# Summing scan blocks over their states in four column groups of TensorE

## The chip, the cores and the metric

The kernel runs on one core of a Trainium2 chip. The metric is device time in microseconds (us), the median of several runs. A core has TensorE (PE; PEld is its weight load), VectorE (DVE), ScalarE (ACT), GpSimd (POOL) and SyncE (SP), which issues most DMAs. Each engine works through its own instructions in order and waits on semaphores for the others.

## The reference, cut to what matters

The program is two layers: a hybrid of a state space model, convolutions and attention, and then an attention layer with a mixture of experts. The change concerns only the selective scan in the first layer, done for four channel groups `nb` of each of four images `b`:

```python
def selective_scan(u, dt, Bm, Cm, A, Dp):
    dA = jnp.exp(dt[..., None] * A)                  # N x 128 channels x 16 states
    dBu = (dt * u)[..., None] * Bm[:, :, None, :]
    def step(h, inp):
        dA_t, dBu_t, C_t = inp
        h = dA_t * h + dBu_t
        return (h, jnp.einsum('bds,bs->bd', h, C_t)) # sum over the 16 states
    ...
    return ys.transpose(1, 0, 2) + u * Dp
```

N is 1024 tokens. For each channel and state a first-order recurrence runs over the tokens; its result is multiplied by C and summed over the 16 states.

## The kernel before, in words

One (nb, b) pair is called a group here, and `order` lists the 16 groups. A group has 128 channels by 16 states, 2048 recurrences; a block is 128 of them (8 channels by 16 states), one per partition, with 1024 tokens along the free dimension. So a group has NJ = 16 blocks and the scan NBLK = 256. Block t is block j = t % 16 of group n = t // 16.

The scan is a loop written out by hand (L808 to L837) in which turn t issues, in this order:

- DVE: the product of dBu with B (L813), then the recurrence into a buffer `hs` (`tensor_tensor_scan`, L816); POOL: `hs` times C, in place (L817)
- in turn j = 2, DVE and POOL close the previous group: `gated` (L479 reads the sum `pY`; L480)
- PE: `select(t + 2)` (L770), which spreads 8 rows of dt * u over 128 partitions into the PSUM tile dBu; there are two such tiles, so it must wait until the recurrence of block t has read the one that it takes
- PE: `add_up(t - 2)` (L778), the sum over states: two matmuls (one for each half of the 1024 tokens) of `hs` with a 128 x 128 matrix of zeros and ones cut out of `strip`. It puts the block's 8 channels into rows 8j to 8j + 7 of `pY`, adds nothing to the other rows, and accumulates over the 16 blocks; `pY` has one PSUM buffer
- SP: `fetch(t + 4)` (L758) brings 8 rows of dt, spread over 128 partitions, into `dA`; ACT: `decay(t + 3)` (L763) makes exp(dt * A) of it
- one of the steps of the next group's preparation, each at its own j: projections on PE (L400 in turns 11 to 14, L411 in turn 0, L457 in turns 8 and 9), activations on ACT, L422 (turn 3) and L429 (turn 5) on DVE, L426, L434, L439 and L444 on POOL
- in turns 6, 7 and 10: `project_out` of the previous group on PE (L487), `store` on DVE (L493), `gate` (L472)

A float32 matmul of 512 columns stands in the trace as two records of PE. The buffers `hs` come from the pool `scan`, of four buffers, so block t takes the buffer of block t - 4; `dA` has five. Before the scan a planner (`Plan`) orders the group norm and layer norm of the four images and the first group's preparation; the images lie in `xs`, of which images 0 and 1 use the four `hs` buffers and images 2 and 3 have tiles of their own in the pool `lnA`. After the scan a second plan runs everything else.

Of the kernel before, what the change touches and what calls it, by code (L numbers as in the profile page):

```python
# [10 lines left out]
F32 = mybir.dt.float32  # L11
# [4 lines left out]
PSUM = bass.MemoryType.PSUM  # L16

B, C, HH, WW = 4, 256, 32, 32
N = HH * WW
NP = N + 2  # L20
P = 128
CT = C // P
NT = N // P
NB, DM, DIN, DS, DTR, K = 4, 64, 128, 16, 4, 4
# [3 lines left out]
DB, XL = P // DS, K - 1  # L28
# [288 lines left out]
def body(tc, g, out):  # L317
    nc = tc.nc
    act, mm = nc.scalar.activation, nc.tensor.matmul
# [3 lines left out]
    def pool(name, bufs, **kw):  # L323
        return tc.tile_pool(name=name, bufs=bufs, **kw)

    with pool("const", 1) as cp, pool("dram", 1, space=bass.MemoryType.DRAM) as drp, contextlib.ExitStack() as late:
# [13 lines left out]
        strip = cst[:, c0 + TT + NTILE + 1 :]  # L340
# [24 lines left out]
        for b in range(B):  # L365
            t = xmp.tile([P, CT, XL + N + 1], F32, tag=f"xm{b}", name=f"xm{b}")
# [3 lines left out]
        NJ = DIN // DB  # L370
        order = [(nb, b) for b in range(B) for nb in range(NB)]
        NBLK = NJ * len(order)
        with pool("mconst", 1) as mc, pool("front", 1) as fp, pool("dts", 2, space=bass.MemoryType.DRAM) as dsp, pool(
# [119 lines left out]
                stt(xb, xb, V("skip")[rows_out], state[n]["po"][rows_out], ALU.mult, ALU.add)  # L493

            state = {}
            with pool("scan", 4) as sp, pool("yps", 1, space=PSUM) as yps, pool("dps", 2, space=PSUM) as dps, pool("lnA", 1) as wp:


                pre = Plan()
# [3 lines left out]
                pre.banks = [t[:, h] for t in first for h in HALVES] + [third[:, 0:512]]  # L503
                pg = third[:, 512 : 512 + 2 * B * CT].rearrange("p (b i k) -> p b i k", b=B, i=2)
                add, pre.spare, pre.slack, pre.split = pre.add, (2, 3), 700, True
                xs = [[sp.tile([P, N], F32, tag="hs", name="hs") for k in range(CT)] for b in range(2)]
                for b in range(2, B):
                    t = wp.tile([P, CT, N], F32, tag=f"xs{b}", name=f"xs{b}")
                    xs.append([t[:, k] for k in range(CT)])
                convr = sp.tile([P, N], F32, tag="dA", name="dA", bufs=5).rearrange("p (t k d) -> p t k d", t=CT, k=K)  # L510
# [241 lines left out]

                dAs, dBus, hss = {}, {}, {}

                def fetch(t):
                    if t < NBLK:
                        dAs[t] = sp.tile([P, N], F32, tag="dA", name="dA", bufs=5)
                        nc.sync.dma_start(out=dAs[t], in_=state[t // NJ]["ds"][t % NJ].unsqueeze(0).to_broadcast([DS, DB, N]))  # L758

                def decay(t):  # L760
                    if t < NBLK:
                        c = order[t // NJ][0] * NJ + t % NJ
                        act(dAs[t], dAs[t], AF.Exp, scale=aneg[:, c : c + 1])  # L763

                def select(t):
                    if t < NBLK:
                        j = t % NJ
                        dBus[t] = dps.tile([P, N], F32, tag="dBu", name="dBu")
                        for h in HALVES:
                            mm(dBus[t][:, h], pick[:, j % 4], state[t // NJ]["U"][:, j // 4, h], start=True, stop=True)  # L770

                def add_up(t):
                    if 0 <= t < NBLK:
                        r, j, hs = state[t // NJ], t % NJ, hss.pop(t)
                        if j == 0:
                            r["pY"] = yps.tile([P, N], F32, tag="y", name="pY")
                        for h in HALVES:
                            mm(r["pY"][:, h], strip[:, P - DB - j * DB : 2 * P - DB - j * DB], hs[:, h], start=j == 0, stop=j == NJ - 1)  # L778

                fronts = [front(n) for n in range(1, len(order))]  # L780
                fronts = [None] + fronts
# [8 lines left out]
                for t in range(4):  # L790
                    add("SP", 900, lambda t=t: fetch(t), ["ds"], [("dA", t)], lag=3000)
                add("ACT", 2400, lambda: decay(0), [("dA", 0), "aneg"], [("dA", 0)])
                add("PE", 1720, lambda: select(0), [("U", q, t) for q in range(3) for t in range(4)] + ["pick"], [("dBu", 0)])
                for t in range(1, 3):
                    add("ACT", 1150, lambda t=t: decay(t), [("dA", t), "aneg"], [("dA", t)])
                add("PE", 1720, lambda: select(1), [("U", q, t) for q in range(3) for t in range(4)] + ["pick"], [("dBu", 1)])
                with pre.beside(-1, -1, low=True):
                    for b in range(1, B):
# [8 lines left out]
                with tc.manual_schedule():  # L807
                    for t in range(NBLK + 9):  # L808
                        n, j = t // NJ, t % NJ
                        if t < NBLK:  # L810
                            r = state[n]
                            dBu = dBus.pop(t)
                            tt(dBu, dBu, r["B"], ALU.mult)  # L813

                            hs = hss[t] = sp.tile([P, N], F32, tag="hs", name="hs")
                            nc.vector.tensor_tensor_scan(hs, dAs.pop(t), dBu, 0.0, ALU.mult, ALU.add)  # L816
                            nc.gpsimd.tensor_tensor(hs, hs, r["C"], ALU.mult)  # L817
                        if j == 2 and n > 0:
                            gated(n - 1)
                        select(t + 2)  # L820
                        add_up(t - 2)
                        fetch(t + 4)
                        decay(t + 3)
                        for ahead in (1, 2):
                            if n + ahead < len(order):
                                for i, step in fronts[n + ahead]:
                                    if i == j - (ahead - 1) * NJ:
                                        step()
                        for i, step in behind:
                            if i == t:  # L830
                                step()
                        if n > 0 and j == 6:
                            project_out(n - 1)
                        if n > 0 and j == 7:
                            store(n - 1)
                        if n < len(order) and j == 10:
                            gate(n)  # L837
# [13 lines left out]
        with pool("sets", 1) as wp, pool("work", 1) as kp, pool("ps2", 1, space=PSUM) as ps:  # L851
# [830 lines left out]
            def experts(plan, *parts):  # L1682
# [20 lines left out]
                for j, (t, i, w) in enumerate(order):  # L1703
# [62 lines left out]
                    if adds:  # L1766
                        adds.pop()()
                    adds.append(add_up)
                adds.pop()()

# [41 lines left out]
            for i in range(B * NT + 2):  # L1812
                b, unit = i // NT, (i - 2) // HT
# [25 lines left out]
        with pool("fin", 3) as fp, pool("rows", 1) as yp, pool("pfin", 4, space=PSUM) as pf:  # L1839
# [5 lines left out]
            for u in range(2 * B):  # L1845
                b, half = u // 2, u % 2
# [20 lines left out]
```

## Time and profile before

| What | us |
|---|---|
| median of three runs (3322.93 to 3326.98) | 3326.42 |
| the profiled execution, its own time | 3332.46 |
| its span, first to last instruction | 3330.7 |
| the scan, first L816 to the end of the last | 104.4 to 1197.8 |
| busy in the span: PE, DVE, ACT, POOL | 2907, 2077, 1513, 1223 |
| busy in the scan: PE, DVE, ACT, POOL | 891, 957, 573, 775 |

The page gives for each group of instructions the line, the engine, the operation, what is written from what, the shapes and the count; behind the bar stand busy time in us and the mean of one in ns; behind the second bar the idle time of the engine just before them, with what ended it. "DVE hs L816 <- PE pY L778" reads: DVE stood before L816 until PE had finished an instruction of L778. PEclk is the granted clock of TensorE as a share of full speed; over the scan it is 0.93.

### The profile page before, as it was taken

How to read it: one execution, taken by the hardware profiler on the slowest of the kernel's cores; microseconds unless marked ns; L12 is line 12 of the kernel's file. 1: busy time of each engine (PE TensorE's matmuls, PEld its weight loads, DVE VectorE, ACT ScalarE, POOL GpSimd, SP SyncE). 2: the span in 40 equal slices, each digit the busy share in tenths (PEclk: the TensorE clock that was granted, in tenths of full speed). 3: DMA queues.
4: the chain of work that ended last, by engine and by line, in shares of the span. 5: the costliest groups of instructions: out<-in, count | busy, mean ns of one | idle time of the engine just before them, and what ended most of it. 6: DMA issues, size and time to landing. Idle time of an engine off the chain costs nothing. (4 is left out here: it accounts for less than half of the span.)

```text
span 3330.7 us, 38748 instructions
## 1 busy us (share of the span) xinstructions
PE 2907.4 (87%) x15274; PEld 1693.4 (51%) x15274; DVE 2077.2 (62%) x2347; ACT 1513.0 (45%) x2086; POOL 1223.0 (37%) x763
## 2 busy tenths in 40 slices
PE   7787788878888668998889989989899999899997
PEld 4333333333333224555555554655555656689996
DVE  5789888888888954746496478557364445511112
ACT  3646445554455423545673574565443333311111
POOL 0677767667767730000000010000002222556662
PEclk7899999998999988999999989999999999999998
DMA  3566555656557630000000000000000000465455
GB/s 125 133 159 160 152 145 149 167 145 156 143 150 170 153 113 0 1 1 1 26 1 1 26 1 1 1 14 1 1 13 7 13 7 14 117 193 131 117 124 157
DMA packets 92872, 265.50 MB, mean 80 GB/s; under 512 B 18182, under 2 KB 36086, under 8 KB 89360
## 3 DMA queue, kind: packets, MB, share of 16 engines
q1 hardware_dynamic: 64000, 198.46, 22.7%
q0 software_dynamic: 26512, 60.35, 7.1%
q10 hardware_dynamic: 2176, 4.19, 0.3%
q8 instruction: 121, 1.98, 0.2%
q14 instruction: 63, 0.52, 0.1%
HBM read 291.70 MB, written 42.80 MB: 100 GB/s over the span
## 5 line engine op out<-in xcount | busy, mean ns | idle before, releaser
L817 POOL TENSOR_TENSOR hs<-hs,bc 128x1024 f32<-128x1024 f32 x256 | 602.1, 2357 | 277.1 <-DVE hs L816 276.9
L816 DVE TENSOR_TENSOR_SCAN hs<-dA,dBu 128x1024 f32<-128x1024 f32 x256 | 585.4, 2287 | 73.8 <-PE pY L778 44.0
L778 PE MATMUL pY<-hs,const 128*128 128x512 f32 x1024 | 530.1, 643 | 15.6 <-DVE u L479 12.8
L763 ACT ACTIVATE dA<-dA,aneg 128x1024 f32<-128x1024 f32 x256 | 287.4, 1144 | 331.6 <-DMA dA<-ds 331.1
L1082 DVE TENSOR_REDUCE nm<-s 128x1 f32<-128x1024 f32 x256 | 301.6, 1219 | 203.4 <-PE s L1077 202.7
L1087 ACT ACTIVATE pr<-s,nm 128x1024 f32<-128x1024 f32 x256 | 284.9, 1116 | 196.9 <-DVE nm L1082 194.7
L1101 PE MATMUL k<-const,pr 128*128 128x128 f32 x2048 | 301.1, 291 | 72.8 <-ACT pr L1087 49.1
L1172 POOL TENSOR_TENSOR b<-b,misc 128x1024 f32<-128x1024 f32 x16 | 36.4, 2299 | 893.3 <-DVE misc L1168 835.0
L1101 PEld LDWEIGHTS k<-const,pr 128*128 128x128 f32 x2048 | 234.1, 147 | 191.8 <-issue 82.4
L770 PE MATMUL dBu<-U,pick 96*128 96x512 bf16 x512 | 162.7, 401 | 186.3 <-DVE hs L816 182.4
L813 DVE TENSOR_TENSOR dBu<-dBu,bc 128x1024 f32<-128x1024 f32 x256 | 311.8, 1218 | 4.0 <-PE dBu L770 3.9
L778 PEld LDWEIGHTS pY<-hs,const 128*128 128x128 f32 x1024 | 208.4, 205 | 204.4 <-issue 165.6
L1077 PE MATMUL s<-b,b 32*128 32x512 f32 x1024 | 286.9, 648 | 3.3 <-ACT pr L1087 3.3
L1107 ACT COPY pT<-k 128x512 f32<-128x512 f32 x320 | 175.8, 593 | 173.0 <-PE k L1101 171.8
L1742 PE MATMUL s<-pT,b 128*128 128x128 f32 x1920 | 230.0, 276 | 3.4 <-DMA b<-we,intse 2.9
L1742 PEld LDWEIGHTS s<-pT,b 128*128 128x128 f32 x1920 | 226.1, 192 | 8.6 <-ACT pT L1745 4.0
L770 PEld LDWEIGHTS <-pick 96*128 96x128 bf16 x512 | 41.8, 99 | 370.3 <-issue 303.6
L1107 DVE COPY pT<-k 128x512 f32<-128x512 f32 x192 | 131.6, 686 | 99.7 <-PE k L1101 85.4
L1746 DVE TENSOR_TENSOR pT<-pT,s 128x512 f32<-128x512 f32 x72 | 49.4, 687 | 228.2 <-ACT pT L1745 228.1
L1121 PE MATMUL k<-pT,b 128*32 128x128 f32 x4096 | 152.2, 290 | 17.9 <-DVE pT L1107 14.8
L1121 PEld LDWEIGHTS k<-pT,b 128*32 128x32 f32 x4096 | 113.1, 115 | 74.4 <-issue 31.1
L1077 PEld LDWEIGHTS s<-b,b 32*128 32x128 f32 x1024 | 102.4, 190 | 91.8 <-issue 76.5
(434 smaller groups left out, 4430.4 us busy)
## 6 DMA issues: line engine op xcount, KB each, us to landing
dA<-ds SPq DMA_DIRECT2D x256, 512.0 KB, 4.8
dq<-parts SPq DMA_DIRECT2D x15, 768.0 KB, 3.3
U<-dq SPq DMA_DIRECT2D x45, 256.0 KB, 4.1
ds<-dt SPq DMA_DIRECT2D x16, 512.0 KB, 3.0
b<-x SPq DMA_DIRECT2D x4, 1024.0 KB, 7.2
acc<-pr SPq DMA_DIRECT2D x8, 512.0 KB, 5.8
xm<-x SPq DMA_DIRECT2D x4, 1024.0 KB, 5.0
tokens<-pr SPq DMA_DIRECT2D x8, 512.0 KB, 2.9
```

The lines of the kernel that those rows point to most:

```text
L763: act(dAs[t], dAs[t], AF.Exp, scale=aneg[:, c : c + 1])
L778: mm(r["pY"][:, h], strip[:, P - DB - j * DB : 2 * P - DB - j * DB], hs[:, h], start=j == 0, stop=j == NJ - 1)
L813: tt(dBu, dBu, r["B"], ALU.mult)
L816: nc.vector.tensor_tensor_scan(hs, dAs.pop(t), dBu, 0.0, ALU.mult, ALU.add)
L817: nc.gpsimd.tensor_tensor(hs, hs, r["C"], ALU.mult)
L1077: mm(S[i][:, HALVES[h]], qT[rr, qt * P : (qt + 1) * P], kT[rr, HALVES[h]], start=True, stop=True)
L1082: "DVE", 1220, lambda i=i, u=u: nc.vector.tensor_reduce(nms[u], S[i], AX.X, ALU.max, negate=True),
L1087: "ACT", 1330, lambda i=i, u=u, hd=hd: act(prs[u % 4], S[i], AF.Exp, bias=nms[u], scale=1.0, accum_out=rss[b % 2][:, k, qt, hd : hd + 1]), ...
L1101: nc.tensor.transpose(bank.t[:, j * P : (j + 1) * P], prs[u][:, c0 : c0 + P], ident)
L1107: lambda dst=dst, bank=bank, on_act=on_act: (nc.scalar.copy if on_act else nc.vector.tensor_copy)(dst, bank.t),
L1121: mm(bank.t[i * HD : (i + 1) * HD, 0:P], v[:, 4 * jh + j, hd * HD : (hd + 1) * HD], pTs[m][jh][:, i, j * P : (j + 1) * P], start=j == 0, s ...
L1742: mm(p12[:, a, c], wbufs[w][:, o : o + P], xT[:, k], start=k == 0, stop=k == CT - 1)
```

## The change

It has three parts. The sum over states is done for four blocks at once: `add_up` does nothing until the fourth block of a set, and then issues eight matmuls (two halves, four blocks), each with 32 columns of `strip` instead of 128, written to the 32 rows of `pY` that belong to block i of the set. Matmuls to different 32-row strips of the output stand in different column groups of TensorE. For that, the blocks of a set must lie 32 channels apart, so blocks are worked off in the order 0, 4, 8, 12, 1, 5, 9, 13 and so on (`which`), and `fetch`, `decay` and `select` take their rows, scales and selections in that order. Since the results of a set must all be kept until then, the pool `scan` has six buffers instead of four; the two more hold image 2 during the norm, in place of its own tile.

`add_up(t - 2)` is still called in turn t, so a set is issued in turns j = 1, 5, 9 and 13 and covers blocks t - 5 to t - 2. Block t + 1 takes the buffer of block t - 5. Ten lines are added ahead of the loop, so L813, L816, L817, L763, L770, L758 and L778 become L823, L826, L827, L767, L774, L762 and L785.

```diff
-            with pool("scan", 4) as sp, pool("yps", 1, space=PSUM) as yps, ...
+            with pool("scan", 6) as sp, pool("yps", 1, space=PSUM) as yps, ...
...
-                xs = [[sp.tile([P, N], F32, tag="hs", name="hs") for k in range(CT)] for b in range(2)]
-                for b in range(2, B):
+                xs = [[sp.tile([P, N], F32, tag="hs", name="hs") for k in range(CT)] for b in range(B - 1)]
+                for b in range(B - 1, B):
...
+                def which(t):
+                    return t % 4 * 4 + t % NJ // 4
+
                 def fetch(t):
                     if t < NBLK:
                         dAs[t] = sp.tile([P, N], F32, tag="dA", name="dA", bufs=5)
-                        nc.sync.dma_start(out=dAs[t], in_=state[t // NJ]["ds"][t % NJ].unsqueeze(0).to_broadcast([DS, DB, N]))
+                        nc.sync.dma_start(out=dAs[t], in_=state[t // NJ]["ds"][which(t)].unsqueeze(0).to_broadcast([DS, DB, N]))
                 def decay(t):
                     if t < NBLK:
-                        c = order[t // NJ][0] * NJ + t % NJ
+                        c = order[t // NJ][0] * NJ + which(t)
                         act(dAs[t], dAs[t], AF.Exp, scale=aneg[:, c : c + 1])
                 def select(t):
                     if t < NBLK:
-                        j = t % NJ
+                        j = which(t)
                         dBus[t] = dps.tile([P, N], F32, tag="dBu", name="dBu")
                         for h in HALVES:
                             mm(dBus[t][:, h], pick[:, j % 4], state[t // NJ]["U"][:, j // 4, h], start=True, stop=True)
                 def add_up(t):
-                    if 0 <= t < NBLK:
-                        r, j, hs = state[t // NJ], t % NJ, hss.pop(t)
-                        if j == 0:
+                    if 0 <= t < NBLK and t % 4 == 3:
+                        r, q = state[t // NJ], t % NJ // 4
+                        four = [hss.pop(t - 3 + i) for i in range(4)]
+                        if q == 0:
                             r["pY"] = yps.tile([P, N], F32, tag="y", name="pY")
                         for h in HALVES:
-                            mm(r["pY"][:, h], strip[:, P - DB - j * DB : 2 * P - DB - j * DB], hs[:, h], start=j == 0, stop=j == NJ - 1)
+                            for i in range(4):
+                                mm(
+                                    r["pY"][32 * i : 32 * i + 32, h], strip[:, P - DB - q * DB : P - q * DB + 32 - DB], four[i][:, h],
+                                    start=q == 0, stop=q == 3,
+                                )
```

More of the change, by code (lines that the diff above doesn't have):

```diff
@@ L495, in body @@
             state = {}
-            with pool("scan", 4) as sp, pool("yps", 1, space=PSUM) as yps, pool("dps", 2, space=PSUM) as dps, pool("lnA", 1) as wp:
+            with pool("scan", 6) as sp, pool("yps", 1, space=PSUM) as yps, pool("dps", 2, space=PSUM) as dps, pool("lnA", 1) as wp:
                 pre = Plan()
```

## The prediction

> **What bounds the kernel now.** I read the page's engine table first (PE 87%, DVE 62% of a span of 3330.7 us), then its forty slices: up to slice 15 DVE stands at 8 or 9 tenths while PE moves between 7 and 8. That is the scan, from 104.4 us (first scan instruction) to 1197.8 us (end of the last): 1093.4 us for 256 blocks, the only stage the change touches. Its groups:
>
> ```profile
> L816 DVE TENSOR_TENSOR_SCAN hs<-dA,dBu 128x1024 f32<-128x1024 f32 x256 | 585.4, 2287 | 73.8 <-PE pY L778 44.0
> L778 PE MATMUL pY<-hs,const 128*128 128x512 f32 x1024 | 530.1, 643 | 15.6 <-DVE u L479 12.8
> L813 DVE TENSOR_TENSOR dBu<-dBu,bc 128x1024 f32<-128x1024 f32 x256 | 311.8, 1218 | 4.0 <-PE dBu L770 3.9
> ```
>
> DVE's two instructions per block make an undisturbed pace of 3.54 us (scans at 699.74 and 703.29 us in the timeline). PE's add_up costs 1.72 us of streaming per block (four records 0.43 us apart). The waits of DVE in the stage say what PE does to that pace:
>
> ```profile
> DVE hs L816 <- PE pY L778: 44.0, 72, 1.6
> DVE xm L493 <- PE mm L487: 32.4, 15, 3.7
> DVE dt L429 <- POOL dt L426: 15.6, 15, 1.2
> DVE u L479 <- PE pY L778: 6.0, 8, 1.7
> ```
>
> So DVE is the bound and PE is close behind it: about 82 us are lost to PE. The timeline shows where. In turns 13, 14, 15, 0, 1 of a group (turn = loop index j; 16 turns are one group) PE runs select, add_up and a projection back to back, 4.17 us a turn, and the scan waits 0.65 us for the add_up of four blocks earlier:
>
> ```profile
> 643.23 0.60 PE L770 MATMUL dBu<-U,pick 96*128 96x512 bf16 x2
> 643.67 1.88 PE L778 MATMUL pY<-hs,const 128*128 128x512 f32 x4
> 645.49 1.98 PE L400 MATMUL mm<-xm,m_cu 64*128 64x512 f32 x4
> ```
> ```profile
> 645.76 2.29 DVE L816 TENSOR_TENSOR_SCAN hs<-dA,dBu 128x1024 f32<-128x1024 f32 x1 [0.65 <-PE pY L778]
> ```
>
> **Do four column groups really run at once?** The attention's L1121 already does this: 16 matmuls of 32 columns over four groups, two records each.
>
> ```profile
> 1376.37 1.08 PE L1121 MATMUL k<-pT,b 128*32 128x128 f32 x32 [0.78 <-DVE pT L1107]
> ```
>
> 32 records in 1.08 us; L1101, full width with the same 128 moving columns, takes 1.04 us for 8. Four at once, then. A set of eight 32-column matmuls over 512 columns (16 records) costs as much PE time as four records now: 1.88 us for four blocks instead of 7.5. PE loses 192 x 1.72 = 330 us of work. I take full concurrency; the other end, 16 records of 0.43 us in a row, is a rival below. [...]
>
> **What is added: a wait of the scan for the newest set.** Sets are issued in turns 1, 5, 9, 13, behind select(t+2) in PE's queue. That select waits for the scan of turn t, whose dBu buffer it takes. A set covers blocks t-5 to t-2, and with six buffers the scan of turn t+1 takes the buffer of block t-5. So in turns 2, 6, 10, 14 scan, select, set, scan is one chain, where before an add_up had two turns of slack. Behind the waiting scan stands all of DVE, the bound. The first matmul's two halves are first and fifth of eight, and groups advance together, so the buffer is free only as the set ends.
>
> Price at full clock, from the end of scan t: select starts 0.05 later (618.86, 618.91), the set 0.44 after that (643.23, 643.67), a change of array shape adds 0.10 (L400's 1.98 against 1.88), the set takes 1.88, and the scan starts 0.21 after PE's end (645.55, 645.76): 2.68 us. Undisturbed it starts after 1.26. **1.42 us** each. At half clock a record lasts 1061 instead of 592 ns, so the set takes some 3.6, the first record starts 0.81 after the select (609.38, 610.19), the shape change costs 0.2: 4.87 us, **3.6 us** each. In turn 6 L429 and its wait for POOL put the scan 3.5 us after the last one anyway: 0 or 1.4.
>
> **Which clock?** The granted clock goes by stretches of 3.41 us. Columns: stretch, length, busy of PE, PEld, DVE, ACT, POOL, PEclk, DMA.
>
> ```profile
> 602.34:605.76 3.42, 1.91 (x6) 0.78 (x6) 3.39 (x3) 3.42 (x4) 3.15 (x2) 1.00 0.22 50
> 605.76:609.17 3.41, 1.26 (x3) 0.28 (x2) 3.28 (x3) 3.36 (x4) 1.40 (x1) 1.00 0.52 156
> 609.17:612.59 3.42, 3.21 (x5) 1.45 (x5) 3.29 (x3) 1.93 (x2) 3.18 (x2) 0.50 0.54 150
> 612.59:616.00 3.41, 2.83 (x8) 1.05 (x7) 2.18 (x3) 1.15 (x1) 3.41 (x2) 1.00 0.02 4
> ```
>
> After a stretch with PE busy under some 1.3 us the next is at half clock (1.26 above; 0.50, 0.77, 0.10 and 1.27 elsewhere); 1.91 and 2.22 keep it. A half-clock stretch must be nearly full (3.21) to end; 2.79 was not enough (from 697.92). Before, every turn has 2.15 us of PE work. After, turns 2, 3, 4, 7 and 15 have the select alone, 0.43 us. Projections (four records, 1.7 us) stay in turns 0 (L411), 6 (L487), 8 and 9 (L457), 10 (L472) and 11 to 14 (L400). [...] The rows above decide: a stretch with 1.26 us of work lost the clock.
>
> So by place:
> - Set of turn 13: turns 10 to 12 are busy, full clock: 14 x 1.42, and 2 x 3.6 where no projection is left (groups 14, 15). 27.1.
> - Set of turn 5, after three empty turns: half clock, 15 x 1.25 (1.4 less the phases where a boundary helps), and 3.6 in group 15, which has no L429. 22.4.
> - Sets of turns 1 and 9, each behind one projection (turn 0 or 8) that follows an empty turn. In about half of the phases of the 3.41 us grid it runs wholly at half (select and projection 4.3 us, longer than the turn) and the set starts late, 2.8 to 3.1; otherwise 1.4 to 1.9. I take 2.3: 29 x 2.3 and 2 x 3.6 in group 15. 73.9.
>
> Together **+123** for 63 waits. **Gains:** the 44.0 and 6.0 go, since PE has no backlog, and some 4 us of scattered waits of L816 and L813. Of the 32.4 half stays: before, select, add_up and L487 stood between two scans; after, select and L487, mostly at half clock, end 4.6 us after the scan, and L493 wants it at 3.5: 15 x 1.1 left, 16 saved. **-70.** The last set drains at half clock, 3.6 instead of 1.98: +2. **Net +55 us.**
>
> Edits at nothing: fetch, decay and select keep number, size and engine (256 transfers of 512 KB on SP's queue, from other rows of the same ds); three of four selects reload equal weights, 0.10 us each, beside PE's idle. Two more hs buffers hold x of batch 2 until POOL's L653 is through at 118.5 us; scans 4 and 5 come at 130 and 134 us. POOL's part of block t-2 ends 1.3 us or more before the scan of turns 1, 5, 9, 13 does, so a set does not wait for it. Uncovered it would cost its lateness, 16 times for each such turn. After the scan the instruction order of every engine is unchanged.
>
> **Rivals.**
> - *Full clock at the sets.* For it: the projections, and a set itself, may fill enough of the stretches. 48 unshielded waits x 1.42 = 68 against all 86 gained: -18, **3308**. It decides below 1.8 us per wait (86/48): faster under that, slower over it. This is the mechanism on the other side; partly true it ends up to no change.
> - *Half clock everywhere.* Against it: turns 9 to 14 are dense. 48 x 3.6 + 15 x 1.4 = 194, gains 54: +140, **3466**.
> - *Groups one after another.* Against it: L1121. The wanted buffer is free after ten records: 5.1 us, 3.8 per wait, 48 x 3.8 + 15 x 1.6 = 206, gains about 50: +156, **3482**.
> - *The wait is hidden after all*, relief without a price: -86, **3240**. Against it: the chain has one order only.
>
> **How the numbers follow.** The profiled execution took 3332.5 us (span 3330.7); the median of the runs is 3326.4, 6.1 less. 3332.5 + 55 - 6.1 gives **3381** against the median; the rivals' times are on that footing too. Chances: forecast 0.60, full clock 0.20, half clock 0.12, one after another 0.05, hidden 0.03. The range, 3312 to 3460, takes in the forecast, most of the full-clock case on its way to no change, and the half-clock case nearly to its end. A measurement of this kernel can tell 0.2% (6.7 us) from no change: faster 0.16 (full clock 0.13, hidden 0.03), same 0.07, slower 0.77.
>
> **What would show it.** In the changed profile: the add-up group near 110 to 170 us busy instead of 530; the scan idle before PE pY in 63 places for 120 us or so, mostly 1.4 to 3.6 each, in turns 2, 6, 10, 14; other turns at 3.54; PEclk lower in the scan than 0.93; L493's wait halved. Wrong if the idle time before the scan is under 70 us (clock stays up) or if 16 records take 6.9 us (no concurrency).

## The result, and the profile after

The changed kernel takes 3437.24 us (median of four runs, 3433.83 to 3440.58) against 3324.68 for the kernel before: 1.034 of its time, interval 1.0322 to 1.0358, or 112.6 us more. The direction is the one forecast, and so is the chain that costs the time; the loss is twice the forecast +55 us. The profiled execution took 3433.83 us, 101.4 more than the profiled execution before (3332.46, above the median of its kernel). The scan now runs from 97.1 to 1297.3 us: 1200.2 instead of 1093.4, so 106.8 us are lost in it. (It also begins 7.3 us earlier, which no step covers. In the other kernels below it begins between 96.2 and 102.7; I did not look for the cause.)

The page of the changed kernel, the granted clock in forty slices and three groups of the scan:

```profile
PEclk8666666667666656899999999999999999999998
...
L826 DVE TENSOR_TENSOR_SCAN hs<-dA,dBu 128x1024 f32<-128x1024 f32 x256 | 585.3, 2286 | 208.8 <-PE pY L785 184.1
...
L823 DVE TENSOR_TENSOR dBu<-dBu,bc 128x1024 f32<-128x1024 f32 x256 | 310.0, 1211 | 2.9 <-PE dBu L774 2.8
...
L785 PE MATMUL pY<-hs,const 128*32 128x512 f32 x1024 | 183.8, 839 | 5.4 <-POOL hs L827 5.4
```

The sum over states now takes 183.8 us of PE instead of 530.1, and still the scan stands idle before it for 184.1 us instead of 44.0. The scan lies in the second to the fifteenth slice. The same row of the page before is

```profile
PEclk7899999998999988999999989999999999999998
```

so the clock in the scan's slices fell from 9 and 8 tenths to mostly 6; over the whole stage it fell from 0.93 to 0.65. The waits of DVE in that stage, changed kernel:

```profile
DVE hs L826 <- PE pY L785: 184.1, 63, 6.4
DVE dt L429 <- POOL dt L426: 18.8, 15, 1.3
DVE xm L493 <- PE mm L487: 16.7, 14, 1.2
```

The wait of L493 is halved, from 32.4 us, as forecast, and that of L479 is gone from the stage (6.0 us before).

There are 63 waits of the scan for a set, as counted beforehand, and all stand in turns 2, 6, 10 and 14. Added up from the timeline by the turn whose set is waited for, against the forecast:

| Set of turn | Waits | Forecast, us | Measured, us | Mean |
|---|---|---|---|---|
| 1 and 9 | 31 | 73.9 | 73.4 | 2.4 |
| 5 | 16 | 22.4 | 19.7 | 1.2 |
| 13 | 16 | 27.1 | 91.1 | 5.7 |
| all | 63 | 123.4 | 184.2 | 2.9 |

So the waits exceed the forecast by 61 us, and the set of turn 13 alone by 64. Set against the 106.8 us lost, the gains in the scan are 184.2 - 106.8 = 77 us, where 70 were forecast. A second profile of the same kernel (the last of the experiments) gives 66.1 us for turns 1 and 9, 19.6 for turn 5 and 90.5 for turn 13 (one more wait there, of 6.0 us, is put down to ACT): the first of them varies, the last stays large.

This is a set of turn 13 in PE's timeline (start, length, work), changed kernel, turns 10 to 13 of group 7:

```profile
678.61 1.98 PE L472 MATMUL mm<-xm,m_in 64*128 64x512 f32 x4
681.56 1.01 PE L774 MATMUL dBu<-U,pick 96*128 96x512 bf16 x2 [0.96 <-DVE hs L826]
682.93 3.78 PE L400 MATMUL mm<-xm,m_cu 64*128 64x512 f32 x4 [0.36 <-ACT sz L474]
686.64 1.03 PE L774 MATMUL dBu<-U,pick 96*128 96x512 bf16 x2
687.60 3.78 PE L400 MATMUL mm<-xm,m_cu 64*128 64x512 f32 x4
691.31 1.03 PE L774 MATMUL dBu<-U,pick 96*128 96x512 bf16 x2
692.28 3.05 PE L785 MATMUL pY<-hs,const 128*32 128x512 f32 x16
695.26 1.98 PE L400 MATMUL mm<-xm,m_cu 64*128 64x512 f32 x4
```

and the scan behind it in DVE's timeline:

```profile
686.30 2.29 DVE L826 TENSOR_TENSOR_SCAN hs<-dA,dBu 128x1024 f32<-128x1024 f32 x1
...
695.52 2.29 DVE L826 TENSOR_TENSOR_SCAN hs<-dA,dBu 128x1024 f32<-128x1024 f32 x1 [5.81 <-PE pY L785]
```

The projections L400 of turns 11 and 12 take 3.78 us instead of 1.98: half clock. With its select such a turn costs PE 4.7 us, while DVE needs 3.54, so PE falls behind: the scan before the wait ends at 688.59, the select that waits for it starts at 691.31, 2.7 us late, the set 1.0 us after that, and the set, half of it at half clock, takes 3.05 us and ends at 695.33; the next scan starts 0.2 us later. That is 6.9 us from the end of one scan to the start of the next, where 2.7 were forecast for full clock and 1.26 is the undisturbed value.

### The profile page after: what moved, and what is told of

The parts are those of the page before. It is cut to its first block, busy times and chain, and to the rows that moved or that the text cites. A ratio compares the mean times of both kernels' runs of the same rounds, so it can differ in the third digit from the quotient of the medians.

```text
span 3432.0 us, 38731 instructions
## 1 busy us (share of the span) xinstructions
PE 2785.5 (81%) x15274; PEld 1548.4 (45%) x15274; DVE 2068.1 (60%) x2347; ACT 1516.7 (44%) x2086; POOL 1221.1 (36%) x763
## 3 DMA queue, kind: packets, MB, share of 16 engines
q10 hardware_dynamic: 2176, 4.19, 0.3%
q8 instruction: 121, 1.98, 0.3%
## 5 line engine op out<-in xcount | busy, mean ns | idle before, releaser
L827 POOL TENSOR_TENSOR hs<-hs,bc 128x1024 f32<-128x1024 f32 x256 | 602.7, 2354 | 428.5 <-DVE hs L826 424.4
L826 DVE TENSOR_TENSOR_SCAN hs<-dA,dBu 128x1024 f32<-128x1024 f32 x256 | 585.3, 2286 | 208.8 <-PE pY L785 184.1
L774 PE MATMUL dBu<-U,pick 96*128 96x512 bf16 x512 | 229.6, 545 | 417.2 <-DVE hs L826 417.0
L767 ACT ACTIVATE dA<-dA,aneg 128x1024 f32<-128x1024 f32 x256 | 290.1, 1146 | 415.7 <-DMA dA<-ds 392.9
L774 PEld LDWEIGHTS <-pick 96*128 96x128 bf16 x512 | 42.5, 106 | 671.4 <-DVE hs L826 378.1
L823 DVE TENSOR_TENSOR dBu<-dBu,bc 128x1024 f32<-128x1024 f32 x256 | 310.0, 1211 | 2.9 <-PE dBu L774 2.8
L1117 DVE COPY pT<-k 128x512 f32<-128x512 f32 x192 | 131.4, 685 | 99.6 <-PE k L1111 86.2
L785 PE MATMUL pY<-hs,const 128*32 128x512 f32 x1024 | 183.8, 839 | 5.4 <-POOL hs L827 5.4
L400 PE MATMUL mm<-xm,m_cu 64*128 64x512 f32 x240 | 170.7, 847 | 7.1 <-ACT sz L474 7.1
```

The lines of the kernel that those rows point to most:

```text
L1117: lambda dst=dst, bank=bank, on_act=on_act: (nc.scalar.copy if on_act else nc.vector.tensor_copy)(dst, bank.t),
```

## The experiments

Theory 1 (as forecast): the loss is the chain scan, select, set, scan; so a kernel in which the set does not stand in that chain loses nothing. Theory 2 (formed on the trace after): the clock weighs TensorE's work by the rows in use, so that the 64-row projections don't keep it up; that makes the set of turn 13 so late. The rivals: the new order of blocks or the two extra buffers cost the time; or matmuls of 32 columns do less for the clock than matmuls of 128. Edits are against the changed kernel. Each interval stands beside the kernel before on the same chip; since the part after the scan took 2133 to 2154 us on the different chips with the same instructions, the length of the scan stage compares kernels better.

| Kernel | Time against before | Scan stage, us | Scan's wait for the sum, us (times) | Clock in the whole span |
|---|---|---|---|---|
| before | 1 | 1093.4 | 44.0 (72) | 0.940 |
| changed | 1.034 | 1200.2 | 184.1 (63) | 0.841 |
| set ahead of select | 1.014 | 1133.2 | 111.4 (41) | 0.857 |
| seven buffers | 0.9991 | 1085.8 | 27.0 (14) | 0.867 |
| each block alone, 128 wide | 1.0005 | 1090.2 | none | 0.941 |
| each block alone, 32 wide | 1.010 (one run) | 1126.6 | none | 0.937 |
| all rows | 1.0224 | 1156.2 | 133.0 (60) | 0.871 |
| kept busy | 1.0128 | 1128.2 | 91.4 (48) | 0.925 |
| set ahead, all rows | 1.0168 | 1136.5 | 107.9 (32) | 0.873 |
| set a turn earlier | 0.9993 | 1088.1 | 27.8 (16) | 0.875 |
| a turn earlier, all rows | 0.9926 | 1067.6 | 6.8 (14) | 0.886 |

### Each block alone, 128 wide

Order of blocks and six buffers as changed; the sum of each block as before.

```diff
-                    if 0 <= t < NBLK and t % 4 == 3:
+                    if 0 <= t < NBLK:
+                        r, j, hs = state[t // NJ], which(t), hss.pop(t)
...
+                            mm(r["pY"][:, h], strip[:, P - DB - j * DB : 2 * P - DB - j * DB], hs[:, h], start=t % NJ == 0, stop=t % NJ == NJ - 1)
```

> The changed kernel without its third part: block order 0, 4, 8, 12, 1 and the six buffers stay, but every block is added up alone and at once, over 128 columns as before. Theory 1 (sets alone cost): as the kernel before or a little faster, since two more buffers give the scan slack: 3300 to 3330 us. Rival (the order or the buffers cost, by the rows fetched or the norm ahead of the scan): above 3340.

Measured: 3344.52 us, 1.0005 of before (0.9988 to 1.0022). The order and the buffers together cost nothing; the loss comes from summing four blocks at once. The little gain that the expectation saw as possible did not come: the scan's 44.0 us of waits for the sum are gone, but the product ahead of it now waits 28.2 us for late selects (2.2 before). PE's backlog shows in another place.

### Each block alone, 32 wide

The same, with 32 columns into the 32 rows of `pY` that belong to the block.

```diff
+                        r, q, i, hs = state[t // NJ], t % NJ // 4, t % 4, hss.pop(t)
...
+                            mm(r["pY"][32 * i : 32 * i + 32, h], strip[:, P - DB - q * DB : P - q * DB + 32 - DB], hs[:, h], start=q == 0, stop=q == 3)
```

> As the kernel where every block is added up alone, but over the 32 columns of its own column group, so that one group works at a time. PE's time in the matmuls is the same at a given clock. Theory 2 in its full form (the throttle counts rows times columns): a turn counts 0.3 + 0.25 x 1.7 us, far under the threshold, PE falls to half clock through most of the scan and becomes the bound, 3600 us or more. If only rows count, or only time: as the wide one, 3300 to 3340.

Measured, in one run: 3376.98 us beside 3343.31. The clock in the whole span stays at 0.937 of full with a quarter of the columns (0.941 with all of them), so that rival falls. The sum takes as much PE time as at full width (the page of this kernel):

```profile
PEclk7899999999999988899999989999999999899998
...
L783 PE MATMUL pY<-hs,const 128*32 128x512 f32 x1024 | 534.1, 650 | 16.9 <-POOL hs L825 13.5
```

With the set of 1.9 us this shows once more that the four column groups of a set do run at once: the same 1024 records take 534.1 us one group after another, and 183.8 us in sets although only 20 of the sets run wholly at full clock. The 1% lost here is PE's: against the 128-wide kernel DVE's waits for selects grow from 28.2 to 42.4 us, those for L487 from 33.4 to 46.7. In the timeline a turn with a projection takes 4.19 to 4.28 us (selects at 645.15, 649.34, 653.62 and 657.90 us) instead of 4.17; from the select to the sum it is 0.53 us instead of 0.44.

### Seven buffers

The scan of turn t + 1 then takes the buffer of block t - 6, which the set before has released; the newest set's first buffer is wanted a turn later. The tile `pickf` lies elsewhere to make room.

```diff
-            with pool("scan", 6) as sp, pool("yps", 1, space=PSUM) as yps, ...
+            with pool("scan", 7) as sp, pool("yps", 1, space=PSUM) as yps, ...
...
-                pickf = wp.tile([96, 32 // DB, P], F32, tag="pickf", name="pickf")
+                pickf = fp.tile([P, N], F32, tag="sz", name="sz")[:96, 0:512].rearrange("p (j q) -> p j q", q=P)
```

> One edit: seven hs buffers instead of six, so the scan that needs a set's first buffer is a turn later (3.54 us of slack); to make room the tile pickf, used before the scan alone, lies in the tile sz. Theory 1: a set at half clock ends 4.9 us after the scan it follows and is wanted at 4.8, so the waits in turns 2, 6, 10 go and of the 5.7 us in turn 14 some 2 us stay: 3270 to 3310 us. Rival (cost of the sets, not of the wait): 3415 or more.

Measured: 3335.11 us, 0.9991 of before (0.9973 to 1.0009); the scan stage is 114 us shorter than in the changed kernel. Turns 2 and 10 are back at 3.51 to 3.54 us. The loss was the wait for the buffer, which is theory 1. But the kernel is no faster than before, so the expectation was missed, though the sum takes PE 350 us less (179.8 instead of 530.1). DVE's waits in the scan say why:

```profile
DVE dBu L823 <- PE dBu L774: 28.9, 36, 1.1
DVE hs L826 <- PE pY L785: 27.0, 14, 2.5
```

PE is still late, with its select (27.7 of the 28.9 us stand in turns 14, 15 and 0) and in turn 15 with the set. That follows on the half clock of turns 10 to 13, which a buffer does not cure: in group 1 the products of turns 14 and 15 start at 232.18 and 236.85 us, 4.67 us apart, about the 4.7 us of a projection and a select at half clock in the changed kernel. The expectation counted only some 2 us a group for it.

### Set ahead of select

```diff
-                        select(t + 2)
                         add_up(t - 2)
+                        select(t + 2)
```

> One edit to the changed kernel: in each turn the set of eight matmuls is issued ahead of select instead of behind it. Theory 1 (the loss is the chain scan, select, set, scan): the set no longer stands behind a select that waits for the newest scan, so it starts a turn earlier and ends before the scan that needs its buffer; the 184 us of idle time before the scan fall to under 50 us (what stays is turn 13, where PE is late from the projections at half clock), about 3260 to 3300 us. Rival (the sets themselves, or the lower clock, are what costs, wherever they stand): no change beyond 20 us, 3415 or more.

Measured: 3383.61 us, 1.014 (1.0102 to 1.0178). Of the waits 111.4 us are left, so the expectation failed. PE's timeline of this kernel, turns 12 and 13 of group 3:

```profile
372.10 1.04 PE L774 MATMUL dBu<-U,pick 96*128 96x512 bf16 x2
373.06 3.77 PE L400 MATMUL mm<-xm,m_cu 64*128 64x512 f32 x4
376.77 3.64 PE L785 MATMUL pY<-hs,const 128*32 128x512 f32 x16
```

The set no longer waits for the newest scan, but it stands behind the projection of the turn before, which at half clock takes 3.77 us, and is itself at half clock. The scan of turn 14 waited 4.95 us for it. In turn 10 the same happens behind L457; in five groups the trace puts that wait, 9.8 us in all, down to ACT, whose work had ended before.

### All rows

The projections L400 and the gate L472 multiply all 128 rows, 64 of them with zero weights, so the sums are the same. Preparing these weights adds some work ahead of the scan, and two tiles used there alone (`m_in`, `pickf`) lie elsewhere to make room.

```diff
-                        mm(r["pu"][:, h], m_cu[rows_in, nb // 2, k], xb[:, k + h.start : k + h.stop], start=k == 0, stop=k == K - 1)
+                        mm(r["pu"][:, h], m_cu[:, nb // 2, nb % 2, k], XM[b][:, nb // 2, k + h.start : k + h.stop], start=k == 0, stop=k == K - 1)
...
-                    mm(p[:, h], m_in[rows_in, nb // 2, DIN:], xb[:, XL + h.start : XL + h.stop], start=True, stop=True)
+                    mm(p[:, h], m_z[:, nb // 2, nb % 2], XM[b][:, nb // 2, XL + h.start : XL + h.stop], start=True, stop=True)
```

> One edit: the projections L400 and the gate L472 use all 128 rows of the array, the other channel group's 64 rows with zero weights, instead of 64 rows; number, length and order of the matmuls in the scan stay, the weights are spread out before it. Theory 2 (the throttle counts how much of the array works, so a 64-row matmul counts half, and turns 10 to 13 fall to half clock for that reason): those turns stay at full clock, the wait of 5.7 us before the scan of turn 14 falls to 1.4 to 2.5, about 50 to 60 us less, 3375 to 3390 us. Rival (the throttle counts time in which PE is busy, and the set of turn 13 is late for another reason): the same time as the changed kernel within 10 us, 3437.

Measured: 3411.32 us, 1.0224 (1.0184 to 1.0263). The step that this was to test came out as theory 2 has it: the waits for the set of turn 13 went from 91.1 us to 29.5, and the forecast, which took full clock there, had 27.1. Two tables of stretches (stretch, length, busy PE, PEld, DVE, ACT, POOL, PEclk, DMA share, GB/s) show the clock in turns 10 to 13. First the changed kernel:

```profile
677.54:680.96 3.42, 2.58 (x6) 0.86 (x6) 3.29 (x3) 3.40 (x4) 2.71 (x2) 1.00 0.51 145
680.96:684.37 3.41, 2.46 (x4) 0.93 (x4) 3.28 (x3) 3.37 (x4) 3.41 (x2) 0.50 0.28 108
684.37:687.78 3.41, 3.41 (x6) 0.64 (x5) 3.28 (x3) 2.01 (x2) 3.03 (x2) 0.50 0.50 163
687.78:691.20 3.42, 3.42 (x4) 0.99 (x4) 1.93 (x2) 0.00 (x0) 2.35 (x1) 0.50 1.03 235
691.20:694.61 3.41, 3.41 (x15) 0.72 (x18) 0.00 (x0) 0.00 (x0) 0.00 (x0) 0.50 1.04 228
694.61:698.02 3.41, 2.79 (x13) 0.86 (x6) 2.50 (x2) 2.29 (x2) 0.13 (x1) 1.00 0.84 197
```

Then the kernel with all rows:

```profile
585.19:588.60 3.41, 1.68 (x5) 0.58 (x4) 3.28 (x3) 3.36 (x4) 3.19 (x3) 1.00 0.35 88
588.60:592.02 3.42, 3.42 (x6) 1.29 (x5) 3.29 (x3) 2.65 (x3) 3.28 (x2) 0.50 0.52 208
592.02:595.43 3.41, 3.41 (x22) 0.91 (x20) 2.58 (x2) 0.00 (x0) 2.22 (x2) 1.00 1.00 231
```

In the first, PE is busy for 2.58 us of a stretch, with a select and the 64-row gate, and the next is at half clock all the same. It stays there through two stretches in which PE is busy for 3.41 and 3.42 us, mostly with 64-row work, and returns after the one that holds the set, which uses all rows. In the second it returned after one stretch of 128-row work (3.42 us).

The whole gained less than the expectation, though. The scan stage is 44 us shorter, but the waits for the sets of turn 1 rose from 32.2 us to 49.8 (three more, of 4 us each, are put down to ACT). That set stands behind L411 of turn 0 (L414 in this kernel), which waits for ScalarE; the section on the set ahead of select with all rows shows it.

### Kept busy

Another way to hold the clock up: products of zeros, added to dBu in the turns with little work. The result is unchanged.

```diff
+                LOAD = (0, 0, 2, 2, 2, 0, 0, 2, 0, 0, 1, 1, 1, 0, 1, 2)
...
+                        if t + 2 in dBus:
+                            for h in HALVES[: LOAD[j]]:
+                                mm(dBus[t + 2][:, h], ones, zero, start=False, stop=True)
```

> The changed kernel with matmuls of zeros added into dBu behind the set and the projection: two full-size ones in turns 2, 3, 4, 7, 15, one in turns 10, 11, 12, 14, so that every turn gives the array work. The result stays. Theory 2: the clock stays full at nearly all sets, each wait before the scan falls to about 1.4 us (0 in turn 6), 184 us of idle time to 70 to 100, 3310 to 3350 us in spite of more work on PE. Rival (the clock is not what makes the sets long): no gain, 3430 or more.

Measured: 3382.44 us, 1.0128 (1.0096 to 1.0159). The clock in the scan rises from 0.65 to 0.90, and DVE's waits there are

```profile
DVE hs L829 <- PE pY L788: 91.4, 48, 3.7
DVE dBu L826 <- PE dBu L853: 19.2, 32, 2.9
```

In turn 6 one of sixteen waits is left, as forecast for full clock. The shortest waits of turns 10 and 14 are 1.46 and 1.57 us, so the forecast price of 1.42 was right for full clock. The mean stays at 1.9, because the clock is not at full in every set (0.90 over the scan), and the added products cost 19.2 us of waits of their own. That is why the kernel stayed above its expectation.

### Set ahead of select, all rows

> The edits of the two kernels with the set ahead of select and with all rows in the projections together. If theories 1 and 2 both hold nothing is left of the waits on PE before the scan but a few us: 62.6 us of undisturbed work per group, some 80 to 90 us under the kernel before, 3235 to 3260 us. If only the first holds: as the set ahead of select alone. If neither: 3415 or more.

Measured: 3393.68 us, 1.0168 (1.0129 to 1.0207), far from the expectation. Turn 14 is good (one wait for PE, of 0.2 us, and five for POOL, of 1.4). In turn 10 the scan still waits 34.2 us in all: the set of turn 9 stands behind the projection of turn 8, which by my reading runs at half clock (turn 0's below takes 3.78 us). And in turn 2 the scan now waits 73.5 us in all. PE's timeline of this kernel there:

```profile
683.82 3.78 PE L414 MATMUL mm<-u,m_wdt 128*128 128x512 f32 x4 [3.87 <-ACT u L407]
687.52 2.20 PE L793 MATMUL pY<-hs,const 128*32 128x512 f32 x16
```

And ScalarE's:

```profile
675.76 1.15 ACT L775 ACTIVATE dA<-dA,aneg 128x1024 f32<-128x1024 f32 x1 [9.31 <-DMA dA<-ds]
677.98 1.15 ACT L775 ACTIVATE dA<-dA,aneg 128x1024 f32<-128x1024 f32 x1 [1.07 <-DMA dA<-ds]
680.19 1.15 ACT L775 ACTIVATE dA<-dA,aneg 128x1024 f32<-128x1024 f32 x1 [1.06 <-DMA dA<-ds]
681.36 1.28 ACT L407 ACT_TABLE_LOAD   x1
682.65 1.11 ACT L407 ACTIVATE u<-mm,vec 128x1024 f32<-128x1024 f32 x1
```

The projection of turn 0 waits 3.87 us for the silu (L407), which stands in ScalarE's queue behind three decays that wait for their transfers: from 670.8 to 684.4 us the DMA engines of this kernel are taken up (share 1.00 to 1.05). Behind the projection stands the set, and behind the set the scan, 5.97 us. My reading, which no run tests by itself, is that in the changed kernel the long wait of turn 14 gave the transfers time, and that they are what is late once it is gone. What was gained in turn 14 was given back in turn 2.

### Set a turn earlier, and with all rows

`add_up(t - 1)` puts a set into turns 0, 4, 8 and 12: it gets one more turn before its first buffer is wanted, and stands ahead of that turn's projection and so ahead of the projection's wait.

```diff
                         select(t + 2)
-                        add_up(t - 2)
+                        add_up(t - 1)
```

> One edit to the changed kernel: add_up is called with t - 1, so each set is issued a turn earlier, in turns 0, 4, 8, 12, still behind select but ahead of that turn's projection; six buffers. Theory 1: the scan that needs the first buffer comes 3.54 us later than the set's turn, so the waits of turns 2, 6 and 10 go as with seven buffers; what stays is PE late after turns 10 to 13 at half clock, some 3 us per group. About as the kernel before or up to 30 us less, 3300 to 3345 us on a chip where that one takes 3340. Rival (the set's place in the queue does not matter as long as it is a set): as the changed kernel, over 3420.

> The set a turn earlier and all 128 rows in the projections and the gate. Theories 1 and 2 together: turns 10 to 13 stay at full clock, the set of turn 0 stands ahead of L411 with its wait for ScalarE (now line L414), and a group comes near its undisturbed 62.6 us: 64 to 66 us, 40 to 75 us less than the kernel before (3265 to 3300 where that takes 3340). If theory 2 is wrong or another wait takes over (the DMA of U, ScalarE's silu): as the set a turn earlier alone.

Measured: 3329.1 us, 0.9993 of before (0.9981 to 1.0006), and with all rows 3304.88 us, 0.9926 (0.9907 to 0.9944). The first does what seven buffers did. The second also brings the projections of turns 12 to 14 back to 1.88 to 1.98 us (PE's timeline, 703 to 712 us) and beats both kernels, by 23.6 us against before and by 131.4 against the changed one (3436.29 on that chip). It is less than the 40 to 75 us of the expectation: a group takes 66.7 us of the scan, not 64 to 66. DVE's two longest waits for PE in its scan:

```profile
DVE dBu L831 <- PE dBu L782: 19.8, 26, 1.4
DVE xm L496 <- PE mm L490: 16.8, 15, 1.3
```

The scan's wait for the sum is down to 6.8 us in 14 waits; its wait for the decays of ScalarE, 13.2 us in 9, is now longer. The clock over this scan is 0.77, below the 0.93 of before: many sets still run at half clock (a set takes 3.0 us on the mean: 193.2 us for 64), but the scan hardly waits for them.

### The changed kernel again

> The changed kernel as it is, beside the two others on one chip, for a base: 1.034 times the kernel before.

Measured: 3436.29 us, 1.0324 (1.0299 to 1.035), on the chip of the last two kernels.

## Why the prediction was right in its chain and wrong in one term

- *Four column groups at once:* right. Sets take 1.93 us at full and 3.64 at half clock (1.88 and 3.6 forecast). The group of the sum is 183.8 us, above the 110 to 170 foretold. That range did not fit the forecast's own terms, which with about half of the sets at 3.6 us come to some 180.
- *The chain and its 63 waits:* right in place and number. Shown by seven buffers and by the set a turn earlier, which take the chain apart and with it 112 to 114 us of the scan stage. Each of them also gives the late set of turn 13 a turn more.
- *The price:* 1.42 us at full clock (1.46 to 1.58 in the kept-busy kernel), 3.6 at half (3.72 in the last groups of the changed kernel): right.
- *Set of turn 5, sets of turns 1 and 9:* 19.7 and 73.4 us against 22.4 and 73.9. The two prices behind one projection were right (in turn 10 some 3.0 us in groups 0 to 8 and 1.7 to 1.9 in groups 9 to 14; 2.8 to 3.1 and 1.4 to 1.9 forecast). How often each would come was a guess, and that the sum agrees to 1% is partly luck: the second profile has 66.1.
- *Set of turn 13:* this is the step that failed: "turns 10 to 12 are busy, full clock: 14 x 1.42". These turns are busy with 64-row matmuls, and those neither kept the clock (half clock came after the stretch at 677.54 us, with PE busy for 2.58 us) nor brought it back (after 3.41 and 3.42 us of busy PE the next stretch was at half clock again). Groups 0 to 13 wait 83.6 us there, 6.0 each, where 19.9 were forecast: +64 us, more than all of the excess in the waits (61). Between the two profiled executions the forecast 55 and these 61, less the 7 gained beyond the forecast and the 7.3 of the earlier start, make 101 us; 101.4 were measured. With all rows the term becomes 29.5 us against the 27.1 of the forecast. I had read a bound of some 1.3 us of busy time off stretches of the kernel before, in which every turn holds 128-row work of the sum. There a bound in busy time fits nearly as well as one weighted by rows: of the stretches at full clock in the scan, 34 of the 35 that were followed by half clock have PE busy for at most 1.31 us, and the 243 that were not have at least 1.43. The step to a kernel without that work went beyond what those rows could tell. The sizes were in view: L400 and L472 read 64x512.
- *Why 5.7 and not 3.6:* at half clock a projection and a select (4.7 us) are longer than a turn, so the set starts late too. I had this for the sets behind one projection, and the rival with half clock everywhere priced only the set itself.
- *Gains:* 77 us in the scan against 70. The 44.0 us before the sum went; turn 8 (behind L493) is 15.8 us shorter over the sixteen groups where 16 were forecast.
- *Rivals:* full clock at the sets would need waits of 68 us; even with the clock held up at 0.90, 91.4 us were left and holding it cost more. "One after another" and "hidden" are excluded by the 1.93 us of a set and by the 63 waits.

Not tried: a kernel in which the sets themselves run at full clock with no product added for it. What the half clock still costs the kernel of 3304.88 us (19.8 us of waits for late selects are left in its scan) stays open.

## What to carry to other kernels

Batching work relieves an engine, but it holds all of a batch's buffers until the last piece is there: ask how many turns lie between the batch and the first buffer that is wanted again, and give the batch a turn of slack (a buffer more, or an earlier issue; here 112 to 114 us of the scan stage) before counting what the engine saves. In an in-order queue the batch belongs ahead of steps that have waits of their own (with all rows, 6.8 us of waits for the sum when the set is issued a turn earlier, ahead of the projection with its wait, and 107.9 behind it). And taking work off an engine can slow what is left: here the clock over the scan fell from 0.93 to 0.65, and a projection of 1.98 us took 3.78. So read from the new kernel's rows, not from the old one's, what still feeds the clock.

## What the runs showed of the hardware

- In the scans of the kernel before and of the changed kernel the granted clock sorts by matmul work weighted by rows; in the changed kernel it does not sort by the time in which PE streams. Take a record of 512 float32 columns as 0.43 us at full clock and twice that at half, from its start on, a select's record as half of it, the four column groups of a set once, and weight each by its rows over 128. Of the stretches of 3.41 us at full clock that lie whole in the scan of the changed kernel, the 57 with at most 0.35 of their length in this work were followed by half clock and the 51 with at least 0.40 were not; before, it was 35 with at most 0.36 and 243 with at least 0.37. The stretch at 677.54 above: four records of 64 rows (4 x 0.43 x 0.5 = 0.86) and the two of a select of 96 rows (0.43 x 0.75 = 0.32) make 1.18 of 3.42 us, 0.35, the most of those that fell. Without the weights the changed kernel has no such bound: stretches with up to 0.63 fell while six with 0.43 to 0.57 stayed. The bound is read off these two traces and was not measured by itself, and the traces do not fix the weight exactly: counting a 64-row record 0.62 instead of 0.5 puts one of the 108 stretches on the wrong side, counting it whole six.
- Matmuls of 32 columns, one block at a time, left the clock at 0.937 in the span (one run), those of 128 columns at 0.941.
- Of the stretches at half clock in the scan of the changed kernel, by the same weighting, the 186 with half clock again behind them had at most 0.77 of their length in this work, and of the 57 after which full clock returned all but one (0.74) had at least 0.78.
